# Three ones-matmul terms instead of four, with later reads and later row tails, in a masked-attention layer

## The chip, the cores and the metric

The kernel runs on one core of a Trainium2 chip. The metric is device time in microseconds (us) of one execution. The core has five engines that run their own instruction queues side by side: PE (TensorE, matrix products), DVE (VectorE), ACT (ScalarE), POOL (GpSimd) and SP (SyncE, which here only starts transfers). Transfers run on 16 DMA engines that all queues share. A transfer that adds into its destination is started by POOL.

## The reference

Eight graphs (F = 8) of 2048 nodes with 256 channels go through one layer of masked attention with 8 heads of 32 channels, then a feed-forward block, and a last residual norm. All is float32. Cut to what matters:

```python
qkv = einsum('fnc,ck->fnk', x, w_qkv)
scores = where(adj > 0, einsum('fnhd,fmhd->fhnm', q, k) / sqrt(D), -1e9)
attn = softmax(scores, axis=-1)
t = einsum('fhnm,fmhd->fnhd', attn, v).reshape(F, N, C)
y = layernorm(x + t, ln1_g, ln1_b)
f_out = relu(y @ w1 + b1) @ w2 + b2
out = layernorm(x + layernorm(y + f_out, ln2_g, ln2_b))
```

The softmax's denominator is the sum of exp(score) over all 2048 nodes m. How that sum is made is what the change is about.

## The kernel before

**Items and groups.** The work is cut into 1024 items `(f, qc, g, mb)`: graph, chunk of 512 query nodes, group of four heads, block of 128 key nodes. The 16 items of one `(f, qc, g)` are called a group here; there are 64. A group with g = 0 is called even, one with g = 1 odd. Item t is step t of the main loop (L552 to L578).

**One step.** PE makes the scores of item t + 2, four matmuls for four heads (L230), into PSUM. DVE adds the mask to them in two halves and writes a tile `p` of 128 x 2048 float32 in SBUF (L233). ACT takes the exponential of item t + 1 in place (L237). PE multiplies the exponentials of item t with the values V and adds the products up over the 16 blocks (L249). Tiles `p` come from a pool of 12.

**The denominator.** The 16 exponential tiles of a group must be summed over blocks and over the 128 nodes of each. PE does the second with a matrix of ones (L310), one "term" of four matmuls for each tile that it is given. To give it few tiles, the tiles are summed first, in `add_up` (L264): blocks 3, 6, 8, 11, 13 and 15 are added into block 0 by POOL (L271, constant `POOLED`); blocks 4, 7 and 10 into block 1, and 5, 9 and 12 into block 2, by accumulating transfers of 1 MB that POOL starts (L268, constant `MOVED`). Block 14 is left as it is (`ALONE`). The heads of these chains and block 14 are four terms. In the very last group, blocks 13 and 15 (`ENDED`) are terms of their own as well. Each addition into a head, by POOL or by a transfer, must wait for the addition before it into the same head.

**Side work.** All else on PE is "side work": generators that yield where they want a PSUM bank (`BANK`), more of the same bank (`MORE`), or a wait of some steps (a positive number). `advance(t)` (L457) runs once a step ahead of the scores. It resumes the generator that holds a bank first, then takes the others in the order of their due times. A credit of 2200 a step against 2048 for a unit of 512 columns in four matmuls means one unit a step, unless the step has reached the due time of something that waits: then it goes on. At most one bank is begun in a step. `start(t, gen, due)` enters a generator with its first step and its due time.

**What the change touches.** `denominator` (L295) reads the terms; it is started two steps after the group's last item and holds back its last term until the step `ready`, four after that item. `outcome` (L328) then divides (L345) and lets a transfer add the input rows to y (L334). `tail` (L349) is started with begin + 10 and due at begin + 26, where begin is six steps after the odd group's last item; it normalises y (`norm`, POOL's small instructions L282 to L286), goes through `feed_forward` (transposes, POOL's L412 and L414, the products with w1 and w2), normalises, multiplies and adds on POOL (L355, L357), adds the input rows by a transfer (L359), normalises and stores. `turn` (L169) loads rows of the next graph, transposes them and stores them as `xd`; `reload` (L191) loads those back. Both wait five steps between the load and its use. `pp` is the pool of `p`, `ld` that of the inputs, of three.

POOL and SP run their instructions in the order of the program: for each step, what `advance` emits comes ahead of what `add_up` emits.

Of the kernel before, what the change touches and what calls it, by code (L numbers as in the profile page):

```python
# [61 lines left out]
def fast_path(ctx, tc, cst, x, adj, out, RS):  # L62
# [106 lines left out]
    def turn(f, c):  # L169
        yield INPUTS - 2  # L170
        xc, xT = take([P, TPC, C], F32), take([P, 2, CH], F32)
        nc.sync.dma_start(xc, x[f, c * CH:(c + 1) * CH, :].rearrange("(j p) c -> p j c", p=P))
        yield 5
        yield from turn_rows(xc, xT)
        give(xc)
        yield 1
        nc.sync.dma_start(XD[f][c], xT)
        XT[f, c] = xT
        give(xT)
# [11 lines left out]
    def reload(f, c):  # L191
        while (f, c) not in XT:
            yield 1
        yield INPUTS - 1
        xT = take([P, 2, CH], F32)
        nc.sync.dma_start(xT, XD[f][c])
        yield 5
        return xT

    def project(f, c, g, xT=None):  # L200
# [19 lines left out]
    PT, O, OT, RC = {}, {}, {}, {}  # L220
# [33 lines left out]

    POOLED = (0, 3, 6, 8, 11, 13, 15)
    MOVED = ((1, 4, 7, 10), (2, 5, 9, 12))
    ALONE = 14

    ENDED = (13, 15)
    SUM = 4

    def add_up(item):  # L264
# [29 lines left out]

    def denominator(f, qc, g, ready):  # L295
        grp = (f, qc, g)
        terms = [PT.pop((f, qc, g, ALONE))] + [PT.pop((f, qc, g, chain[0])) for chain in MOVED + (POOLED,)]
        if (f, qc, g) == items[-1][:3]:
            terms[3:3] = [PT.pop((f, qc, g, b)) for b in ENDED]
        yield BANK  # L300
        ps = bank()
        for n, term in enumerate(terms):
            if n:
                yield MORE
            while n == len(terms) - 1 and state["now"] < ready:
                yield WAIT
            state["credit"] -= 4 * CH
            for h in range(4):
                r = D * h
                nc.tensor.matmul(ps[r:r + D, :], cst["ones"], term[:, h, :], start=(n == 0), stop=(n == len(terms) - 1))  # L310
        dT = op.tile([P, CH], F32, name="dT")
        nc.scalar.copy(dT, ps)
        yield 1
        yield BANK
        ps = bank()
        transposes(ps, [dT[:, j::TPC] for j in range(TPC)])
        if g == 0:
            RC[f, qc] = op.tile([P, TPC, H], F32, name="rc")
        rc = RC[f, qc]
        den = ps.rearrange("p (j c) -> p j c", c=P)[:, :, ::D]  # L320
        nc.vector.reciprocal(rc[:, :, 4 * g:4 * g + 4], den)
        nc.vector.tensor_tensor(RS[:, 0], RS[:, 0], den, ALU.add)
        nc.vector.tensor_tensor(RS[:, 1], RS[:, 1], den, ALU.min)
        if g == 1:
            begin = items.index((f, qc, g, LAST)) + SUM + 2
            start(begin, outcome(f, qc) if (f, qc) != (F - 1, NCK - 1) else finish(f, qc), begin)

    def outcome(f, qc):  # L328
        yield ROOM
        state["tails"] += 1  # L330
        xin = x[f, qc * CH:(qc + 1) * CH, :].rearrange("(p j) c -> p j c", p=P)
        y = yp.tile([P, TPC, C], F32, name="y")
        yield from divide(f, qc, y)
        nc.gpsimd.dma_start(y, xin, accum_op=ALU.add)  # L334
        begin = items.index((f, qc, 1, LAST)) + SUM + 2
        start(begin + 10, tail(f, qc, y, xin), begin + 26)

    def divide(f, qc, y):
        rc = RC.pop((f, qc))
# [62 lines left out]
    def feed_forward(y):  # L402
        yield TURNED
        state["turned"] = True
        yT = work.tile([P, 2, CH], F32, name="turned")
        for a in range(2):
            yield BANK
            ps = bank()
            transposes(ps, [y[:, j, a * P:(a + 1) * P] for j in range(TPC)])
            nc.scalar.activation(yT[:, a, :], ps, AF.Identity, bias=cst["be1c"][:, a:a + 1], scale=cst["g1c"][:, a:a + 1])  # L410
        yield 1
        nc.gpsimd.tensor_tensor(y, y, rows(cst["g1r"]), ALU.mult)  # L412
        yield 1
        nc.gpsimd.tensor_tensor(y, y, rows(cst["be1b2r"]), ALU.add)  # L414
        hT = work.tile([P, 2, CH], F32, name="hT")
        for d in range(2):
            yield BANK
            ps = bank()
            for a in range(2):
                if a:  # L420
                    yield MORE
                columns(ps, w1s[:, a, d * P:(d + 1) * P], yT[:, a, :], start=(a == 0), stop=(a == 1))
            nc.scalar.activation(hT[:, d, :], ps, AF.Relu, bias=cst["b1s"][:, d:d + 1], scale=1.0)
        state["turned"] = False
        yield 1
        z = y
        for jj in range(0, TPC, 2):
            yield BANK
            ps = bank()
            for j in range(jj, jj + 2):  # L430
                if j > jj:
                    yield MORE
                for d in range(2):
                    columns(ps[:, (j - jj) * C:(j - jj + 1) * C], hT[:, d, j * P:(j + 1) * P], w2s[:, d, :],
                            start=(d == 0), stop=(d == 1))
            nc.vector.tensor_tensor(z[:, jj:jj + 2, :], ps.rearrange("p (b c) -> p b c", c=C), z[:, jj:jj + 2, :], ALU.add)  # L436
# [4 lines left out]
    def start(t, gen, due):  # L441
        fill.append([t, gen, 1, due])
        fill.sort(key=lambda e: e[3])
# [108 lines left out]
    for t, (f, qc, g, mb) in enumerate(items):  # L552
        if g == 1 and mb % 2 and (f + 1 < F or qc + 1 < NCK):
            load_mask(f + (qc + 1) // NCK, (qc + 1) % NCK, mb // 2)
        for what, *which in NEXT.get(t % FRAME, []):
            to = f if what is ask and which[0] else f + 1
            if to < F:
                at = (0, 0, 0) if what is turn else (which[0], 0, 0) if what is ask else (0, which[1], which[0] * TPC)
                start(t, what(to, *which), t + 3 * MB if what is turn else items.index((to, *at)) - LEAD - 1)
        if t == len(items) - MB // 2:  # L560
            state["rows"] = take([P, TPC, C], F32)
            nc.sync.dma_start(state["rows"], x[f, qc * CH:(qc + 1) * CH, :].rearrange("(p j) c -> p j c", p=P))
        if t:
            advance(t)

        if t + 1 < len(items):
            exponentials(items[t + 1])
        if t + LEAD < len(items):
            nf, _, ng, nmb = items[t + LEAD]
            t0 = t  # L570
            while (nf, nmb // TPC, ng) not in V:
                advance(t0, finish=True)
                t0 += 1
            scores(items[t + LEAD])
        values(items[t])
        add_up(items[t])
        if mb == LAST:
            start(t + 2, denominator(f, qc, g, t + SUM), t + SUM + 4)  # L578
    t = len(items)
    state["side"] = None  # L580
    while fill:
# [238 lines left out]
```

## Time and profile before

| | us |
|---|---|
| median of 3 runs | 3245.18 (3244.88 to 3248.27) |
| profiled execution, its time | 3242.05 |
| profiled execution, its span | 3240.0 |
| ACT exponentials, busy | 1956.3 |
| DVE mask additions, busy | 2410.5 |
| POOL additions of `p` (382), busy | 1829.5 |
| POOL transfer issues of `p` (384), busy | 360.1 |

The main loop runs from 98 to 3176 us of the span; there PE is busy 3012.0 us of 3078, DVE 2672.4, ACT 2386.0, POOL 2565.7, and the DMA engines have a mean busy share of 0.82. The transfers of POOL's queue take 67.2% of 16 engines' span and move 435.85 MB; SP's take 13.1% and move 149.98 MB. The granted PE clock is 1.00 throughout the loop.

A group row of such a page gives the line, engine and operation, the tiles that are written and read, their shape, the number of instructions, then the busy time and the mean of one in ns, and after the bar the idle time of that engine just ahead of them with what ended it. Matmuls of float32 appear twice in the records, so a term of four matmuls is eight of them. A wait is listed as engine, line, what ended it, the total in us, how often, and the longest.

### The profile page before, as it was taken

What the parts mean: (1) busy time and instruction counts of PE and PEld (TensorE: products, weight loads), DVE (VectorE), ACT (ScalarE), POOL (GpSimd) and SP (SyncE); (2) the same over time, 40 slices, a digit from 0 to 9 for tenths busy, and PEclk for the clock granted to TensorE, in tenths of its full rate; (3) what the DMA queues carried; (4) which work ended last, traced back from release to release, by engine and by line L of the source; (5) the groups of instructions that cost most, each with busy time, mean ns of one, the idle gap of its engine ahead of it and who ended that gap; (6) DMA issues with size and microseconds to landing.
All of it is one profiled execution on the core that took longest, in us unless ns stands there. A gap on an engine that the chain in (4) does not pass through costs nothing.

```text
span 3240.0 us, 68306 instructions
## 1 busy us (share of the span) xinstructions
PE 3101.0 (96%) x28948; PEld 976.0 (30%) x28948; DVE 2739.5 (85%) x3203; ACT 2435.5 (75%) x1937; POOL 2593.3 (80%) x1357
## 2 busy tenths in 40 slices
PE   7899999999999999999999999999999999998994
PEld 4222333323332233322333323323233323332221
DVE  4888888888888888888988888888888888888994
ACT  3667778778778777778777778777778777777773
POOL 0568888788878888788887888888888788878894
PEclk8899999999999999999999999999999999999997
DMA  9688779778879788788788879878788878877773
GB/s 322 147 179 190 182 175 202 176 174 200 181 176 205 171 190 193 158 195 200 177 181 175 184 181 220 177 167 197 175 192 194 180 171 201 181 171 160 168 160 78
DMA packets 153384, 591.57 MB, mean 183 GB/s; under 512 B 15056, under 2 KB 67792, under 8 KB 103920
## 3 DMA queue, kind: packets, MB, share of 16 engines
q0 software_dynamic: 64560, 435.85, 67.2%
q1 hardware_dynamic: 87696, 149.98, 13.1%
q8 instruction: 229, 3.75, 0.4%
q10 hardware_dynamic: 816, 1.31, 0.1%
q14 instruction: 83, 0.68, 0.1%
HBM read 146.67 MB, written 37.75 MB: 57 GB/s over the span
## 4 chain that ended last, share of the span: by engine, by line
PE 75%; DVE 8%; POOL 5%; DMA 4%; issue 4%; ACT 2%; DVEq 0%; ACTq 0%; POOLq 0%
PE s L230 28%; PE x L249 24%; PE x L54 13%; DVE p L233 6%; PE x L310 6%; PE x L95 4%; DMA p<-p 3%; POOL p L271 2%; ACT p L237 2%; DMA mask<-md 1%; POOL y L357 1%; DVE st L278 1%; POOL y L355 0%; POOL y L414 0%; POOL y L412 0%
## 5 line engine op out<-in xcount | busy, mean ns | idle before, releaser
L233 DVE TENSOR_TENSOR p<-s,mask 128x1024 f32<-128x1024 f32 x2048 | 2410.5, 1219 | 360.3 <-PE s L230 202.9
L237 ACT ACTIVATE p<-p 128x2048 f32<-128x2048 f32 x1024 | 1956.3, 1910 | 510.2 <-DVE p L233 456.7
L271 POOL TENSOR_TENSOR p<-p 128x2048 f32<-128x2048 f32 x382 | 1829.5, 4791 | 216.0 <-ACT p L237 213.8
L230 PE MATMUL s<-qT,kT 32*128 32x512 f32 x8192 | 1171.2, 641 | 34.1 <-DVE p L233 29.1
L249 PE MATMUL x<-p,v 128*32 128x512 f32 x8192 | 1092.9, 606 | 16.7 <-ACT p L237 16.7
L268 POOL DMA_DIRECT2D p<-p x384 | 360.1, 957 | 305.5 <-ACT p L237 95.5
L230 PEld LDWEIGHTS s<-qT,kT 32*128 32x128 f32 x8192 | 320.5, 183 | 637.8 <-DVE p L233 580.1
L249 PEld LDWEIGHTS x<-p,v 128*32 128x32 f32 x8192 | 161.3, 108 | 796.4 <-issue 302.6
L310 PE MATMUL x<-p,ones 128*32 128x512 f32 x2016 | 261.1, 594 | 15.9 <-POOL p L271 9.7
L289 ACT ACTIVATE y<-y,nb,rs 128x256 f32<-128x256 f32 x372 | 219.2, 590 | 46.1 <-POOL nb L286 46.1
L54 PE MATMUL x<-in,wqkv 128*32 128x512 f32 x1888 | 243.5, 592 | 0.0
L278 DVE BATCH_NORM_STATS2 st<-y 128x6 f32<-128x256 f32 x372 | 155.2, 417 | 6.2 <-DMA y<-in_x_dram 6.2
L54 PE MATMUL x<-w2s,hT 128*32 128x256 f32 x2048 | 122.8, 381 | 3.3 <-DVE y L436 2.3
L54 PE MATMUL x<-turned,w1s 128*32 128x512 f32 x992 | 122.9, 592 | 0.4 <-ACT in L166 0.4
L54 PEld LDWEIGHTS x<-wqkv,in 128*32 128x32 f32 x3584 | 102.2, 110 | 63.5 <-issue 59.0
L54 PE MATMUL x<-wqkv,in 128*32 128x128 f32 x3584 | 117.2, 273 | 0.0
L310 PEld LDWEIGHTS x<-p,ones 128*32 128x32 f32 x2016 | 64.1, 110 | 171.4 <-issue 136.0
L54 PEld LDWEIGHTS x<-in,wqkv 128*32 128x32 f32 x1888 | 61.7, 110 | 140.9 <-issue 113.7
L283 POOL TENSOR_TENSOR rs<-rs,mhalf 128x4 f32<-128x4 f32 x93 | 97.1, 1044 | 7.7
L54 PEld LDWEIGHTS x<-w2s,hT 128*32 128x32 f32 x2048 | 66.1, 110 | 76.5 <-issue 30.3
L414 POOL TENSOR_TENSOR y<-y,be1b2r 128x1024 f32<-128x1024 f32 x32 | 85.4, 2667 | 0.6
L355 POOL TENSOR_TENSOR y<-y,g2r 128x1024 f32<-128x1024 f32 x31 | 82.7, 2668 | 1.2 <-ACT y L289 1.2
(117 smaller groups left out, 1333.1 us busy)
## 6 DMA issues: line engine op xcount, KB each, us to landing
p<-p POOLq DMA_DIRECT2D x384, 1024.0 KB, 10.5
in<-xd SPq DMA_DIRECT2D x87, 512.0 KB, 10.7
mask<-md SPq DMA_DIRECT2D x248, 128.0 KB, 8.0
y<-in_x_dram POOLq DMA_DIRECT2D x62, 512.0 KB, 8.0
p<-in_adj_dram SPq DMA_DIRECT2D x16, 1024.0 KB, 9.7
out_dram<-y SPq DMA_DIRECT2D x31, 512.0 KB, 6.4
in<-in_x_dram SPq DMA_DIRECT2D x29, 512.0 KB, 15.9
xd<-in SPq DMA_DIRECT2D x28, 512.0 KB, 10.9
```

The lines of the kernel that those rows point to most:

```text
L54: nc.tensor.matmul(out[r:r + D], lhsT[:, r:r + D], rhs, start=start, stop=stop)
L95: nc.tensor.transpose(ps[:, j * P:(j + 1) * P], s, ident)
L230: nc.tensor.matmul(ps2[half][:, j, :], KT[f, mb // TPC, g][r:r + D, (mb % TPC) * P:(mb % TPC + 1) * P], QT[f, qc, g][r:r + D, :], start=Tr ...
L233: nc.vector.tensor_tensor(pt[:, 2 * half:2 * half + 2, :], ps, MK[f, qc, mb // 2][:, mb % 2, None, :].to_broadcast([P, 2, CH]), ALU.add)
L237: nc.scalar.activation(PT[item], PT[item], AF.Exp, scale=1.0 / math.sqrt(D))
L249: nc.tensor.matmul(O[grp][r:r + D, :], V[f, mb // TPC, g][:, mb % TPC, r:r + D], PT[item][:, h, :], start=(mb == 0), stop=(mb == LAST))
L268: nc.gpsimd.dma_start(PT[f, qc, g, chain[0]], PT.pop(item), accum_op=ALU.add)
L271: nc.gpsimd.tensor_tensor(first, first, PT.pop(item), ALU.add)
L278: nc.vector.bn_stats(st, t[:, j, :])
L283: nc.gpsimd.tensor_tensor(rs, rs, cst["mhalf"], ALU.pow)
L289: nc.scalar.activation(t[:, j, :], t[:, j, :], AF.Identity, bias=nb[:, j:j + 1], scale=rs[:, j:j + 1])
L310: nc.tensor.matmul(ps[r:r + D, :], cst["ones"], term[:, h, :], start=(n == 0), stop=(n == len(terms) - 1))
```

## The change

Five things, all of them constants:

- `POOLED` takes block 14 in place of 13; block 13 goes to the end of the chain of block 1, as a fourth transfer of that chain; there is no block alone. The two chains change places in the tuple. `ENDED` is (14, 15).
- `denominator` has three terms, in the order block 2's chain, block 1's chain, block 0's; it starts four steps after the last item and holds its last term until six steps after it. Its due time stays.
- `tail` is due six steps later.
- In `feed_forward`, two steps instead of one between the products with w1 and those with w2.
- The wait between load and use is eight steps in `turn` and six in `reload`.

```diff
@@ turn @@
-        yield 5
+        yield 8
@@ reload @@
-        yield 5
+        yield 6
@@ add_up's constants @@
-    POOLED = (0, 3, 6, 8, 11, 13, 15)
-    MOVED = ((1, 4, 7, 10), (2, 5, 9, 12))
-    ALONE = 14
-
-    ENDED = (13, 15)
+    POOLED = (0, 3, 6, 8, 11, 14, 15)
+    MOVED = ((2, 5, 9, 12), (1, 4, 7, 10, 13))
+
+    ENDED = (14, 15)
@@ denominator @@
-        terms = [PT.pop((f, qc, g, ALONE))] + [PT.pop((f, qc, g, chain[0])) for chain in MOVED + (POOLED,)]
+        terms = [PT.pop((f, qc, g, chain[0])) for chain in MOVED + (POOLED,)]
         if (f, qc, g) == items[-1][:3]:
-            terms[3:3] = [PT.pop((f, qc, g, b)) for b in ENDED]
+            terms[2:2] = [PT.pop((f, qc, g, b)) for b in ENDED]
@@ outcome @@
-        start(begin + 10, tail(f, qc, y, xin), begin + 26)
+        start(begin + 10, tail(f, qc, y, xin), begin + 32)
@@ feed_forward @@
         state["turned"] = False
-        yield 1
+        yield 2
@@ main loop @@
-            start(t + 2, denominator(f, qc, g, t + SUM), t + SUM + 4)
+            start(t + SUM, denominator(f, qc, g, t + SUM + 2), t + SUM + 4)
```

## The prediction

> **What bounds the kernel now.** I read the page first, then the waits of POOL, then the order of time on PE and on POOL, and last the busy shares of short stretches. The page: its first part, the chain that ended last, one group and one DMA row.
>
> ```profile
> PE 3101.0 (96%) x28948; PEld 976.0 (30%) x28948; DVE 2739.5 (85%) x3203; ACT 2435.5 (75%) x1937; POOL 2593.3 (80%) x1357
> ...
> PE 75%; DVE 8%; POOL 5%; DMA 4%; issue 4%; ACT 2%; DVEq 0%; ACTq 0%; POOLq 0%
> ...
> L310 PE MATMUL x<-p,ones 128*32 128x512 f32 x2016 | 261.1, 594 | 15.9 <-POOL p L271 9.7 <-DMA p<-p 6.1
> ...
> p<-p POOLq DMA_DIRECT2D x384, 1024.0 KB, 10.5
> ```
>
> PE is busy 96% and carries 75% of the chain. That names the bound on average, and it is where the change removes work. PE's order of time shows what one removed term is worth:
>
> ```profile
> 1783.57 1.06 PE L249 MATMUL x<-p,v 128*32 128x512 f32 x8
> 1784.46 1.04 PE L310 MATMUL x<-p,ones 128*32 128x512 f32 x8
> 1785.43 1.14 PE L230 MATMUL s<-qT,kT 32*128 32x512 f32 x8
> 1786.50 1.06 PE L249 MATMUL x<-p,v 128*32 128x512 f32 x8
> ```
>
> A step is scores, values and one unit of side work: 2.93 us from score to score (1782.50 to 1785.43), of which scores and values take 2.07 in the merged chain (1.07 and 1.00) and the unit 0.86. But the second bound stands close behind it, and the averages hide it. POOL's waits:
>
> ```profile
> POOL p L271 <- ACT p L237: 213.8, 77, 85.5
> ...
> POOL p L268 <- DMA p<-p: 79.0, 33, 5.4
> ```
>
> The second row matters: a transfer L268 waits for the transfer three or four blocks earlier in its own chain, since both add into the same head, and POOL stands still meanwhile. One group of 16 blocks on POOL (columns: start, duration, what, idle before it):
>
> ```profile
> 1861.91 0.86 POOL L268 DMA_DIRECT2D p<-p  x1 [0.64 <-ACT y L289]
> 1862.47 4.91 POOL L271 TENSOR_TENSOR p<-p 128x2048 f32<-128x2048 f32 x1
> 1871.66 0.88 POOL L268 DMA_DIRECT2D p<-p  x1 [4.28 <-issue]
> 1872.25 2.69 POOL L355 TENSOR_TENSOR y<-y,g2r 128x1024 f32<-128x1024 f32 x1
> 1874.58 4.85 POOL L271 TENSOR_TENSOR p<-p 128x2048 f32<-128x2048 f32 x1
> 1879.11 2.67 POOL L357 TENSOR_TENSOR y<-y,be2r 128x1024 f32<-128x1024 f32 x1
> 1882.08 0.88 POOL L359 DMA_DIRECT2D y<-in_x_dram  x1 [0.30 <-POOL y L357]
> 1882.70 4.86 POOL L271 TENSOR_TENSOR p<-p 128x2048 f32<-128x2048 f32 x1
> 1887.64 0.19 POOL L282 TENSOR_SCALAR rs<-mv 128x4 f32<-128x4 f32 x1
> ...
> 1889.47 4.57 POOL L271 TENSOR_TENSOR p<-p 128x2048 f32<-128x2048 f32 x1
> 1893.97 1.85 POOL L268 DMA_DIRECT2D p<-p  x2
> ```
>
> In order: transfer of block 10, addition of 11, 4.28 us idle, transfer of 12 (block 9 landed at 1871.1), additions of 13 and 15, the next group's addition of 3, its transfers of 4 and 5. The DMA side of the end of it:
>
> ```profile
> core 0: us, PE busy (x) PEld busy (x) DVE busy (x) ACT busy (x) POOL busy (x), PEclk, DMA share, GB/s
> ...
> 1884.00:1887.00 3.00, 2.49 (x20) 0.47 (x16) 2.17 (x3) 1.91 (x1) 3.00 (x1) 1.00 1.01 201
> 1887.00:1890.00 3.00, 2.39 (x20) 0.63 (x24) 1.09 (x2) 1.26 (x2) 2.66 (x6) 1.00 0.20 55
> 1890.00:1893.00 3.00, 3.00 (x28) 1.15 (x24) 2.88 (x6) 2.29 (x3) 3.00 (x1) 1.00 0.00 0
> ```
>
> The DMA engines are full while a group's transfers run, then empty (0.00) until POOL reaches the next transfer of 4. So there is a loop that takes turns between two resources: transfers 4 to 9 on full DMA engines, a wait of POOL for a landing, three additions, transfer of 4 again.
>
> **What the Trainium skill says.** "DMA: Bandwidth & Descriptors", Rules for kernel authors: an accumulating DMA reads its destination and writes it later with nothing held in between, so the earlier DMA's semaphore must be waited for. The 79.0 us row is that wait. The same page, Issuing engines are not separate DMA queues: all run on the same 16 engines; the share of 1.01 above agrees. "TensorE: Matmul & The Clock Gate", Part 1, Architectural detail: GpSimd's queue is strictly first in, first out, so what follows a waiting transfer waits too; the additions behind the 4.28 us agree. "GPSIMD Engine Reference", 3.1: 4497 ns for such an addition; the trace has 4791 (4.5 apart when back to back), and I use the trace's.
>
> **The change part by part.**
>
> Term 14 alone goes: 64 groups lose one unit, 64 x 0.86 = 55 us of PE. Where a step then holds no unit, the two DVE additions of 1219 ns bound it at 2.44, and 0.49 is saved instead. So PE's own floor falls by 31 to 55 us, to about 3190.
>
> Block 13 becomes a transfer: 64 more of 1 MB. The transfers of POOL's queue take 67.2% of 3240 us for 435.85 MB, so 5.2 us for 1.05 MB. DMA share in the loop rises from 0.82 by 64 x 5.2 / 3078 = 0.11 to 0.93. The issue costs POOL 0.6 to 0.96 each (957 mean, 0.6 to the next instruction): 38 to 61 us. POOL's additions stay at six, now with 14 in place of 13.
>
> The new wait is the main point. Transfer 13 adds into head 1 and waits for transfer 10; behind it on POOL stand the additions of 14, 15 and the next 3, then the transfer of 4, which starts the next group's DMA work. Until now the last wait was 12 for 9. In the trace block 10 lands one transfer after 9: 1876.8 against 1871.1. From that landing I count to the next transfer of 4: 0.5 to notice, 0.6 issue, three additions 14.3, plus the tail's work in between.
>
> The tail's place: its due time moves from step 15 of the odd group (LAST + 32) to step 5 of the next even one. Until now w1 and w2 were forced two units a step and w2 ended near step 1; now they go singly, with one step more between them, and w2 ends near step 5. Eleven steps of norm and yields later come L355, L357 and L359: from steps 12 to 15 to steps 16 to 18. In program order that is behind addition 15, out of the wait's cover: 2.3 + 2.7 more. y's transfer (0.6) and the four small ones of a norm (1.9) are between as before. Even group: 0.5 + 0.6 + 14.3 + 5.0 + 0.6 + 1.9 = 22.9. Odd group: L412 and L414 fall before transfer 13, in the wait; 14.9 (additions joined without a DMA: 13.7).
>
> From transfer 4 to block 10's landing the trace has a mean of 34.8 us in even groups (31.1 to 37.8; y's 512 KB is among them) and 32.3 in odd ones (29.6 to 34.6). New loop: 57.7 + 47.2 = 104.9 for two groups. Now it is 49.5 + 47.3 = 96.8. So +8.0 with transfers as traced and the tail where I count it. Two things the trace can't say. SP's loads may move into the gap and shorten the stretch: with the shortest seen, 31.1 and 29.6, two groups take 6.4 less. And I count the tail's steps from the code; if its two multiplications still find cover, 5.0 less. So +8.0 at one end and -3.4 at the other, where PE's own gain of 1.7 for two groups would take over; I take the middle, +2.3. Times 31.5 pairs: +72. Once, about 9 us of lag is taken up before PE waits: the POOLED term is now read 19.0 us after block 15's exponential and its addition ends 10.7 to 12.4 after it, and it moves two steps later. Sum: +63.
>
> The terms start at t + 4 and the last at t + 6. The chain heads are read two steps later (5.9 us), which covers 13's later landing (about 5.7 behind 12's) at today's pace, not an added lag per group. Their buffers come free later; twelve are there, and I count 9 to 11 in use. The longer waits in `turn` (8) and `reload` (6) cost nothing while side work fills every step and inputs are due a dozen steps later. SP's store of xd moves three steps later, and SP's reloads queue behind it; without that cover a block's units are forced, say one 0.86 for each of 28 turned pieces and 87 reloads, 99 us; I take 0. Swapping the chains in MOVED only orders the reads: the chain that ends with 12 first.
>
> Sum against the profiled execution's 3242.05: 3305. The median shown is 3 us higher: 3308.
>
> **The rivals.** (1) The same loop at its worst end: +8.0 x 31.5 - 9 = +243, 3488. For it: the stretch repeats with the position in the frame within 1 us, so its loads are the program's own, and the order on POOL is the program's. Against it: SP's loads have 13.1% of the engines' time and the gap is new room for them. (2) A buffer: block 13's landing, some 6 us later than 12's, gates DVE's write of block 6 of the next group if buffers are handed out in order of release. Priced at 1.5 us a group less PE's gain: 96 - 55, 3286. For it: exponentials end only 1.0 to 1.3 us before values read them. Against it: DVE waits for POOL's transfers 4.3 us in all today. (3) The other side, faster: the wait of 13 is filled by work that POOL must do anyway, so the loop stays under PE's: 3245 - 55 = 3190. It decides from the point where the loop of two groups falls below PE's 96.8 - 1.7 = 95.1; with stretches as traced it is 104.9, so 9.8 us of them, or of the tail's work behind transfer 13, must move. PE's 75% of the chain speaks for it, and the 5 to 7 us for which POOL stands idle between its transfers of 4 and 12, which the tail could use; against it, the shortest stretches seen still give 98.5 with the tail where I count it. (4) The two cancel within 0.2%, which is about 6 us and what a measurement can tell from no change.
>
> **How the numbers follow.** Forecast 0.52 (its own range 3255 to 3400); rival 1 0.16; rival 2 0.10; rival 3 0.16; cancelling 0.06. Slower 0.78, same 0.06, faster 0.16. The range is 3230 to 3445: it leaves out most of rival 3 and the upper part of rival 1.
>
> **What would show it.** POOL's waits for DMA p<-p at L268 grow from 79.0 to 200 us or more, and the idle stands ahead of transfer 13. L310 or DVE begin to wait for POOL and DMA; PE's share falls below 95%; L355 and L357 come after the addition of 15. DMA share near 0.90. It is wrong if L268's waits stay near 79, or if PE stays at 96% with a shorter span: then the gap was covered.

## The result and the profile after

The changed kernel takes 3528.1 us (median of four runs, 3522.6 to 3531.7) against 3246.7 us before on the same chip: a ratio of 1.0865, with a 95% interval of 1.0846 to 1.0884. That is 281 us slower, well above the forecast of 3308 us and above its range, which ended at 3445. The profiled execution's span is 3523.7 us. In the code of the changed kernel the lines from 260 on stand one lower: the transfers are L267, POOL's additions L270, the norm's POOL instructions L281 to L285, ACT's part of the norm L288, the terms L309, the division L344, the tail's multiplication and addition L354 and L356, those of `feed_forward` L411 and L413.

The page of the changed kernel, busy shares, the chain that ended last, the group of the terms and the transfers:

```profile
PE 3134.8 (89%) x28436; PEld 976.2 (28%) x28436; DVE 2732.9 (78%) x3203; ACT 2431.2 (69%) x1937; POOL 2648.1 (75%) x1421
...
DMA 3%; POOL 3%; PE 3%; issue 1%; DVE 1%; ACT 1%; POOLq 0%; ACTq 0%; DVEq 0%
...
L309 PE MATMUL x<-p,ones 128*32 128x512 f32 x1512 | 193.2, 596 | 18.2 <-DMA p<-p 18.1
...
p<-p POOLq DMA_DIRECT2D x448, 1024.0 KB, 10.8
```

PE fell from 96% to 89%, and no other engine rose: ACT and DVE have the same work spread over more time, and POOL, which got 64 issues more, has a smaller share as well. The engines' work has hardly grown; they wait for each other more. The chain that ended last was followed back through some 12% of the span only, so this time it names no bound. The term did go (1512 matmul records for 2016, 193.2 us for 261.1), and a transfer still takes about as long from issue to landing (10.8 us, 10.5 before). The waits of the changed kernel, all engines, say where the time is (engine, line, what ended it, total us, times, longest):

```profile
ACT y L288 <- POOL nb L285: 245.2, 46, 14.4
POOL p L267 <- DMA p<-p: 211.3, 83, 6.7
...
POOL p L267 <- issue: 123.8, 52, 7.4
...
PE x L249 <- ACT p L237: 108.0, 30, 9.5
...
PE s L230 <- DVE p L233: 100.8, 151, 3.3
```

The same waits of ACT and PE before:

```profile
ACT y L289 <- POOL nb L286: 46.1, 16, 9.3
...
PE s L230 <- DVE p L233: 29.1, 65, 1.4
...
PE x L249 <- ACT p L237: 16.7, 11, 5.1
```

Two rows stand out, not one. POOL's wait for landings is the row that the forecast announced (79.0 before). It is not where it was announced: split by block, 4.3 of its 211.3 us stand ahead of transfer 13, the rest ahead of earlier transfers. The wait ahead of 13 is there all the same, listed under other names. Counted from the landings (POOL idle for more than 0.3 us ahead of a transfer that starts within 1 us of the landing before it in its chain), it comes to 194.5 us in 45 of the 64 groups; the wait ahead of 12, the last one before, went from 57.6 to 10.7 us, the one ahead of 10 from 151.5 to 182.3.

The largest row was small before: ACT stands at its part of the norm for POOL's `nb`, 245.2 us against 46.1. ACT takes its instructions in order, so the exponentials stand behind it; PE's wait for them went from 16.7 to 108.0.

**The even groups.** POOL in one even group, in order of time (start, duration, what, idle before it):

```profile
2015.91 1.58 POOL L267 DMA_DIRECT2D p<-p  x1
2024.88 0.85 POOL L267 DMA_DIRECT2D p<-p  x1 [7.39 <-issue]
2025.45 9.52 POOL L270 TENSOR_TENSOR p<-p 128x2048 f32<-128x2048 f32 x2
2034.95 2.35 POOL L354 TENSOR_TENSOR y<-y,g2r 128x1024 f32<-128x1024 f32 x1
2037.37 2.36 POOL L356 TENSOR_TENSOR y<-y,be2r 128x1024 f32<-128x1024 f32 x1
2040.03 0.89 POOL L358 DMA_DIRECT2D y<-in_x_dram  x1 [0.30 <-POOL y L356]
...
2042.81 4.57 POOL L270 TENSOR_TENSOR p<-p 128x2048 f32<-128x2048 f32 x1
2047.33 1.83 POOL L267 DMA_DIRECT2D p<-p  x2
```

The transfer of 12 is issued at 2015.91, and POOL then stands for 7.39 us until block 10 has landed (2024.4 in the records of the transfers; the row puts the wait down to "issue", the same wait under another name). Behind the transfer of 13 come the additions of 14 and 15, both tail instructions, the row transfer, the norm's four small ones, the next group's addition of 3, and only then its transfer of 4. The DMA engines meanwhile, in four stretches of the same time:

```profile
core 0: us, PE busy (x) PEld busy (x) DVE busy (x) ACT busy (x) POOL busy (x), PEclk, DMA share, GB/s
...
2032.00:2036.00 4.00, 3.52 (x32) 0.71 (x24) 3.69 (x5) 3.10 (x2) 4.00 (x2) 1.00 0.99 218
2036.00:2040.00 4.00, 2.18 (x12) 0.52 (x16) 1.00 (x1) 2.25 (x2) 3.65 (x2) 0.70 0.21 67
...
2044.00:2048.00 4.00, 4.00 (x36) 1.36 (x36) 3.34 (x6) 3.78 (x4) 4.00 (x3) 1.00 0.21 41
2048.00:2052.00 4.00, 4.00 (x40) 0.96 (x36) 3.50 (x4) 3.31 (x4) 4.00 (x3) 1.00 1.03 251
```

They are full until 13 has nearly landed (2037.8), almost empty (0.21) while POOL works, but for the 512 KB of the tail's rows in the stretch left out (2040 to 2044), and full again from the transfer of 4. That is the forecast's loop.

**The odd groups.** POOL at the end of an odd group, and ACT at the same time:

```profile
1971.26 0.87 POOL L267 DMA_DIRECT2D p<-p  x1 [0.95 <-ACT p L237]
1971.84 9.43 POOL L270 TENSOR_TENSOR p<-p 128x2048 f32<-128x2048 f32 x2
1981.36 0.19 POOL L281 TENSOR_SCALAR rs<-mv 128x4 f32<-128x4 f32 x1
...
1983.03 0.19 POOL L285 TENSOR_SCALAR nb<-nb 128x4 f32<-128x4 f32 x1
1985.73 4.54 POOL L270 TENSOR_TENSOR p<-p 128x2048 f32<-128x2048 f32 x1 [2.52 <-ACT p L237]
1990.21 1.83 POOL L267 DMA_DIRECT2D p<-p  x2
```

```profile
1968.38 1.91 ACT L237 ACTIVATE p<-p 128x2048 f32<-128x2048 f32 x1 [1.30 <-DVE p L233]
1983.26 0.60 ACT L288 ACTIVATE y<-y,nb,rs 128x256 f32<-128x256 f32 x1 [12.97 <-POOL nb L285]
1983.76 1.89 ACT L237 ACTIVATE p<-p 128x2048 f32<-128x2048 f32 x1
```

Here the last norm of the tail has its POOL part behind the transfer of 13 and both additions. ACT stands 12.97 us for it. After it the roles turn round: POOL stands 2.52 us for the exponential of block 3, which ACT could not make earlier. For a part of this stretch PE does nothing at all:

```profile
1976.00:1980.00 4.00, 1.84 (x20) 0.47 (x12) 2.83 (x4) 0.00 (x0) 3.92 (x2) 0.98 0.94 197
1980.00:1984.00 4.00, 0.00 (x0) 0.00 (x0) 0.33 (x1) 0.74 (x2) 2.88 (x5) 0.88 0.16 33
1984.00:1988.00 4.00, 2.29 (x16) 0.76 (x20) 0.00 (x0) 4.00 (x4) 2.27 (x1) 0.50 0.01 4
```

(The columns are those of the windows above.) From 1980 to 1984 PE is idle and nearly all else too; POOL is busy for 2.88 of the 4.00 us. In the whole trace ACT has 17 such waits of over 5 us, all in odd groups. POOL's wait behind them, for the exponential of block 3, is much rarer: 20.5 us in all over the groups 4 to 59.

### The profile page after: what moved, and what is told of

It is laid out like the page before. It is cut to its first block, busy times and chain, and to the rows that moved or that the text cites. A ratio compares the mean times of both kernels' runs of the same rounds, so it can differ in the third digit from the quotient of the medians.

```text
span 3523.7 us, 67543 instructions
## 1 busy us (share of the span) xinstructions
PE 3134.8 (89%) x28436; PEld 976.2 (28%) x28436; DVE 2732.9 (78%) x3203; ACT 2431.2 (69%) x1937; POOL 2648.1 (75%) x1421
## 5 line engine op out<-in xcount | busy, mean ns | idle before, releaser
L270 POOL TENSOR_TENSOR p<-p 128x2048 f32<-128x2048 f32 x382 | 1831.7, 4797 | 174.0 <-ACT p L237 169.5
L230 PE MATMUL s<-qT,kT 32*128 32x512 f32 x8192 | 1188.2, 650 | 107.2 <-DVE p L233 100.8
L249 PE MATMUL x<-p,v 128*32 128x512 f32 x8192 | 1121.2, 620 | 177.0 <-ACT p L237 108.0
L267 POOL DMA_DIRECT2D p<-p x448 | 426.4, 994 | 548.3 <-DMA p<-p 211.3
L288 ACT ACTIVATE y<-y,nb,rs 128x256 f32<-128x256 f32 x372 | 220.4, 594 | 245.2 <-POOL nb L285 245.2
L54 PE MATMUL x<-in,wqkv 128*32 128x512 f32 x1888 | 244.4, 594 | 0.1
L309 PE MATMUL x<-p,ones 128*32 128x512 f32 x1512 | 193.2, 596 | 18.2 <-DMA p<-p 18.1
L54 PE MATMUL x<-turned,w1s 128*32 128x512 f32 x992 | 142.2, 648 | 0.0
L54 PE MATMUL x<-w2s,hT 128*32 128x256 f32 x2048 | 137.3, 403 | 1.1 <-ACT oT L253 0.7
L54 PE MATMUL x<-wqkv,in 128*32 128x128 f32 x3584 | 121.2, 282 | 15.8 <-DVE y L344 15.8
L54 PEld LDWEIGHTS x<-wqkv,in 128*32 128x32 f32 x3584 | 106.1, 114 | 69.9 <-issue 47.4
L282 POOL TENSOR_TENSOR rs<-rs,mhalf 128x4 f32<-128x4 f32 x93 | 96.1, 1033 | 7.7
L54 PEld LDWEIGHTS x<-in,wqkv 128*32 128x32 f32 x1888 | 61.3, 110 | 142.0 <-issue 121.3
L54 PEld LDWEIGHTS x<-w2s,hT 128*32 128x32 f32 x2048 | 69.8, 117 | 96.3 <-issue 61.6
L309 PEld LDWEIGHTS x<-p,ones 128*32 128x32 f32 x1512 | 48.0, 110 | 136.9 <-issue 94.2
L311 ACT COPY dT<-x 128x512 f32<-128x512 f32 x63 | 36.9, 586 | 68.2 <-PE x L309 68.1
L413 POOL TENSOR_TENSOR y<-y,be1b2r 128x1024 f32<-128x1024 f32 x32 | 82.3, 2573 | 0.6
## 6 DMA issues: line engine op xcount, KB each, us to landing
p<-p POOLq DMA_DIRECT2D x448, 1024.0 KB, 10.8
```

Of the source, the lines that this page charges most:

```text
L54: nc.tensor.matmul(out[r:r + D], lhsT[:, r:r + D], rhs, start=start, stop=stop)
L230: nc.tensor.matmul(ps2[half][:, j, :], KT[f, mb // TPC, g][r:r + D, (mb % TPC) * P:(mb % TPC + 1) * P], QT[f, qc, g][r:r + D, :], start=Tr ...
L249: nc.tensor.matmul(O[grp][r:r + D, :], V[f, mb // TPC, g][:, mb % TPC, r:r + D], PT[item][:, h, :], start=(mb == 0), stop=(mb == LAST))
L267: nc.gpsimd.dma_start(PT[f, qc, g, chain[0]], PT.pop(item), accum_op=ALU.add)
L270: nc.gpsimd.tensor_tensor(first, first, PT.pop(item), ALU.add)
L282: nc.gpsimd.tensor_tensor(rs, rs, cst["mhalf"], ALU.pow)
```

## The experiments

All kernels were timed over four runs (`y_turn_only` over twelve) beside the kernel before; ratios are given with their 95% intervals. In the expectations, "loop theory" is the forecast's mechanism; "ACT theory" and, in later ones, "norm theory" mean that ACT's wait for the norm is the cost; "DMA theory" means the fuller DMA engines, and "buffer theory" that tiles are held longer and their next writer waits.

I read every trace in the same way: from the issue of the transfer of 4 to the landing on which the group's last waiting transfer depends, and from that landing to the next group's transfer of 4, as means over the groups 4 to 59. The four legs of a pair add up to its period, so the sum only restates the time (both ends of the run are left out; 31.5 times the difference to the pair before gives the difference of the medians within 26 us); how it is split is the finding.

| kernel | landing of block | even: to landing, to next 4 | odd: to landing, to next 4 | pair | median us |
|---|---|---|---|---|---|
| before | 9 | 28.0, 21.6 | 26.0, 21.4 | 97.0 | 3247 |
| changed | 10 | 31.5, 23.1 | 32.2, 19.2 | 106.0 | 3528 |
| a_tail_back | 10 | 33.6, 19.2 | 31.4, 17.6 | 101.8 | 3390 |
| b_tail_only | 9 | 26.4, 27.6 | 28.1, 23.6 | 105.7 | 3495 |
| n_tail_norm_early | 9 | 25.2, 26.6 | 27.9, 21.6 | 101.3 | 3367 |
| q_changed_norm_early | 10 | 31.4, 22.9 | 32.7, 17.6 | 104.6 | 3481 |
| x_tail_loads_back | 10 | 33.0, 18.9 | 31.2, 15.7 | 98.8 | 3303 |
| w_late13_loads_back | 10 | 33.4, 17.1 | 31.4, 16.0 | 97.9 | 3275 |
| f_behind12 | 12 | 40.1, 19.1 | 38.1, 16.3 | 113.6 | 3754 |

**The tail put back.** The changed kernel with the tail's two times as before:

```diff
-        start(begin + 10, tail(f, qc, y, xin), begin + 32)
+        start(begin + 10, tail(f, qc, y, xin), begin + 26)
...
-        yield 2
+        yield 1
```

> The changed kernel with the tail's due time (begin + 26) and the step between the feed-forward products (1) of before; the three terms and the transfer of block 13 stay. Loop theory (transfer 13 waits for block 10's landing, and all that stands behind it on POOL sets the group's length): the two multiplications go back into the wait's cover, 5.0 us for two groups, 3528 - 157 = about 3370. ACT theory (POOL is late, and the last norm's ACT instructions wait for POOL's nb and hold the exponentials up): the last norm's POOL work falls ahead of transfer 12 again, ACT's wait for nb goes from 245 back to some 50 us, about 3330. DMA theory (the added 1 MB a group fills the DMA engines, and that alone is the price): about 3500 or more.

3390.4 us, ratio 1.0445 (1.0423 to 1.0466). The tail's times are worth 138 us of the 281 here, 4.2 us a pair by the legs; the loop theory had 157 us. ACT's wait for `nb` fell from 245.2 to 84.8 us, POOL's for landings from 211.3 to 117.4. What is left, 145 us, belongs to chains, terms and loads.

**The tail alone.** The kernel before with only these two times changed.

> The kernel before with only the tail's due time (begin + 32) and the two steps between the feed-forward products of the change. Loop theory: the last wait is still 12 for 9, and the multiplications come behind it, 27.5 + 22.9 = 50.4 us against 49.5 in even groups and little in odd ones: 3275 to 3310. ACT theory: the last norm comes behind transfer 12 and its additions, ACT's wait for nb rises by 100 us or more: 3350 to 3450. DMA theory: no transfer is added, 3247.

3495.3 us, ratio 1.0771 (1.0753 to 1.0789). It lies above every range that was named: no transfer of 13, no term less, and still 250 us. So the two halves do not add (145 and 250 against 281 for both). The waits and POOL's order of time of this kernel:

```profile
ACT y L289 <- POOL nb L286: 217.9, 26, 11.8
...
POOL p L268 <- DMA p<-p: 176.6, 51, 6.0
PE x L249 <- ACT p L237: 148.1, 23, 10.4
```

```profile
1955.97 1.01 POOL L268 DMA_DIRECT2D p<-p  x1
1956.56 2.82 POOL L414 TENSOR_TENSOR y<-y,be1b2r 128x1024 f32<-128x1024 f32 x1
1958.88 9.58 POOL L271 TENSOR_TENSOR p<-p 128x2048 f32<-128x2048 f32 x2
1968.55 0.19 POOL L282 TENSOR_SCALAR rs<-mv 128x4 f32<-128x4 f32 x1
```

The norm's first instruction L282 stands behind the transfer of 12 and the additions of 13 and 15, as it does in the changed kernel behind 13, 14 and 15. The later tail brings the same order about without the new chain. In the even groups L355 and L357 stand behind the addition of 15 as well: the stretch from the landing to the next transfer of 4 grew from 21.6 to 27.6 us, in the odd ones from 21.4 to 23.6. DVE writes a tile `p` anew only when the transfer that read it has landed; its wait for that grew as well, from 4.3 to 100.6 us. Whether the pool of 12 tiles is a bound of its own here was not tried.

**The norm's second half later.** The changed kernel with seven steps in place of two between POOL's and ACT's part of the last norm, so that ACT would reach it after `nb` is there:

```diff
-        yield from norm(z)
+        yield from norm(z, 7)
```

> The changed kernel with seven steps instead of two between POOL's nb and ACT's use of it in the last norm of a tail alone; nothing depends on that norm but the store. Loop theory: POOL's order and its waits stay, no gain, 3500 to 3530. ACT theory: of the 245 us that ACT waits for nb, the some 215 that are the last norm's go: about 3310. DMA theory: no gain.

3562.9 us, ratio 1.0976 (1.0956 to 1.0996), slower than the changed kernel. ACT's wait is gone (20.4 us), but the result rows are stored five steps later, and `y` has two buffers:

```profile
DVE y L344 <- DMA out_dram<-y: 95.4, 23, 8.9
```

The next division waits for the store, 95.4 us of it, and DVE's wait for the landings of `p` grew from 51.2 to 141.4 us. One wait was swapped for another, so this run says nothing on what ACT's wait costs.

**The norm's first half earlier.** The other way to part them: the wait ahead of the last norm cut, once on the tail alone and once on the changed kernel.

```diff
         nc.gpsimd.dma_start(z, xin, accum_op=ALU.add)
-        yield 7
+        yield 3
         yield from norm(z)
```

> The kernel before with the tail's two new times (due at begin + 32, two steps between the feed-forward products) and the wait ahead of the tail's last norm cut from 7 steps to 3, so that its four small POOL instructions stand some four steps earlier, ahead of the transfer of block 12 and of the additions of 13 and 15. Norm theory (what the later tail costs is ACT standing at the last norm for POOL's rs and nb, with the exponentials behind it): ACT's wait at L289 for POOL's nb falls from 217.9 us to under 90, and the time from 3495 to 3250 to 3340. Loop theory (the cost is POOL's L355 and L357 behind addition 15): these stay where they are, so the time stays at 3430 to 3500. Buffer theory (y or the exponentials' buffers are held longer whatever the norm does): 3400 to 3500 with ACT's wait gone.

> The changed kernel with the wait ahead of the tail's last norm cut from 7 steps to 3. Loop theory (transfer 13's wait and the tail's multiplications behind addition 15 set 57 us for each even group): the even groups keep their 57 us, and only the odd ones can gain; 3440 to 3520. Norm theory alone: ACT's wait at L288 falls from 245 us to under 110 and the time by about as much, to 3370 to 3430. Both bind together, each in its own group of the pair: ACT's wait falls but the time lands at 3430 to 3480. Buffer theory: no gain, 3500 to 3560.

With the tail alone: 3367.0 us, ratio 1.0370 (1.0348 to 1.0392), 128 us less than 3495.3. The whole last norm stands four steps earlier, with POOL's four instructions of 0.2 to 1.0 us, ACT's part and the store, and half of the tail's cost went. The store is not the reason: nothing waits for it in either kernel with the tail alone. With the whole change: 3481.1, ratio 1.0722 (1.0700 to 1.0744), 47 us less. ACT's waits fell to 61.1 and 50.9 us. The lines of the first, where the tail's cost was larger:

```profile
POOL p L268 <- DMA p<-p: 178.9, 57, 6.5
...
PE s L230 <- DVE p L233: 111.1, 112, 6.6
...
ACT y L289 <- POOL nb L286: 61.1, 22, 8.6
```

POOL's wait for landings is the same as in the tail alone (178.9 and 176.6), and the stretch behind it in the even groups keeps 26.6 of 27.6 us: that half of the cost is not the norm. In the changed kernel the even groups keep 22.9 of 23.1 us, while the odd ones fall from 19.2 to 17.6. So the place of the norm is a cost of its own, in the odd groups, beside the loop in the even ones. Not all of it is ACT's stall: of the 1.6 us, 0.75 are the norm's own time on POOL, which no longer stands behind the landing, and 0.85 are POOL's idle time, nearly all of it the wait for an exponential. Neither theory alone gave both times: the loop theory's 3440 to 3520 holds for the second run but its 3430 to 3500 not for the first, the norm theory missed both. The outcome in which both bind, each in its own group, had 3430 to 3480 for the second, and 3481 is at its upper edge.

**Each half of the tail's delay.** The kernel before with the due time alone, and with the extra step alone.

> The kernel before with the tail due at begin + 32 and nothing else. Norm theory: the due time is what moves the last norm past the transfer of 12 and the additions, so nearly all of the tail's cost is here: 3400 to 3500, ACT's wait for nb 150 us or more. Loop theory: 3275 to 3310. If the extra step between the products is the cost: 3247 to 3270.

> The kernel before with two steps in place of one between the feed-forward products and nothing else. Norm theory: one step moves the last norm only from about steps 11 and 12 to 12 and 13 of the odd group, still ahead of the transfer of 12: 3247 to 3290, ACT's wait for nb under 80 us. If the two parts of the tail's delay simply add (3495 less 3355 from the run with the due time alone): 3380 to 3400.

3355.0 (ratio 1.0329, 1.0311 to 1.0348) and 3336.8 us (1.0279, 1.0254 to 1.0304). Both missed: the due time cost less than the norm theory said, and one single step cost 90 us where next to nothing was expected. ACT's wait is 114.4 us in the first and 93.5 in the second, from 46.1. In the second PE also waits 51.9 us for rows of the next graph that ACT has still to copy (L54 for L166), a sign that the side work changes its order as a whole when one of its generators is shifted. 108 and 90 add to 198 of the 250 us for both.

**Block 13 as a term of its own.** The changed kernel without the seventh transfer; block 13 is read as a fourth term.

```diff
-    MOVED = ((2, 5, 9, 12), (1, 4, 7, 10, 13))
+    MOVED = ((2, 5, 9, 12), (1, 4, 7, 10))
+    ALONE = 13
```

> The changed kernel with block 13 left alone as a fourth term, so with no transfer of 13; POOLED, the later terms and the later tail stay. Loop theory: the last wait is 12 for 9 again: 3275 to 3310. ACT theory: POOL is late by one transfer less, but the last norm still stands behind 12: 3300 to 3400. DMA theory: all of the loss goes, about 3250.

3473.5 us, ratio 1.0705 (1.0687 to 1.0723), above all three ranges. Only 55 us come back, with one term more for PE, and DVE's wait for landings goes from 51.2 to 122.5 us. The time is close to that of the tail alone (3495), which has the same wait of 12 for 9 and the same late tail. So 64 transfers of 1 MB are not the main part of the price, and as long as the tail is late, taking the wait of 13 away leaves most of the loss; the loop theory as I had put it (3275 to 3310) missed here.

**The chains and later terms alone,** with tail and load waits as before, and the same with the transfer of 13 issued behind the addition of 15, its chain read last and one step later:

> The kernel before with the change's chains and later terms alone: tail and both load waits as before. Loop theory with the forecast's own numbers, without the tail's two multiplications: 52.7 + 47.2 = 99.9 us for a pair of groups against 96.8, times 31.5 less 9 = +89, so 3320 to 3350, and POOL's wait for landings at 100 us or more. If transfer 13 is covered: 3190 to 3240. If the chains are the whole cost of the run with the tail put back, and the longer loads cost nothing there: 3380 to 3400.

> The same with the transfer of block 13 issued behind the addition of 15 and its chain read last, one step later. Loop theory: 10 us of additions leave the stretch between block 10's landing and the next transfer of 4, so it falls under PE's pace, and one term per group is saved: 3190 to 3250. If the 64 more transfers cost by themselves, through fuller DMA engines or held buffers: 3260 to 3320, with DVE's wait for landings at L233 at 40 us or more.

```diff
             if mb in chain[1:]:
-                nc.gpsimd.dma_start(PT[f, qc, g, chain[0]], PT.pop(item), accum_op=ALU.add)
+                if mb != 13:
+                    nc.gpsimd.dma_start(PT[f, qc, g, chain[0]], PT.pop(item), accum_op=ALU.add)
...
+        if mb == LAST:
+            nc.gpsimd.dma_start(PT[f, qc, g, 1], PT.pop((f, qc, g, 13)), accum_op=ALU.add)
```

3302.9 us (1.0180, 1.0163 to 1.0197) and 3274.6 (1.0096, 1.0079 to 1.0113). The first is what the forecast was really about: its legs of 18.9 and 15.7 us to the next transfer of 4 were forecast at 17.9 (22.9 less the tail's 5.0) and 14.9, the other two, 33.0 and 31.2, at 34.8 and 32.3, and the period of 98.8 at 99.9. That is a rise of 1.8 us a pair where 3.1 were forecast, and 57 us in all where 3320 to 3350 meant 74 or more. Moving one issue behind two additions, with its chain read last and a step later, took 28 us off, where the loop theory had 3190 to 3250. The time lies in the range for fuller DMA engines or held buffers (3260 to 3320), with DVE's wait below the 40 us that was named for it; neither was tried by itself. The floor of 3190 is not reached by either. In the second DVE waits 33.6 us for landings, PE 66.1 us for DVE and 36.2 us for input rows:

```profile
PE s L230 <- DVE p L233: 66.1, 118, 4.0
...
PE x L95 <- DMA in<-in_x_dram: 36.2, 6, 6.6
...
DVE p L233 <- DMA p<-p: 33.6, 15, 5.0
```

**The same issue moved with the longer loads, and with the whole change.**

> The changed kernel with the tail's two times put back (due begin + 26, one step) and the transfer of block 13 issued after the addition of block 15 rather than ahead of addition 14, its chain read last by the terms and one step later. All bytes and terms of the change stay; only POOL's wait for block 10's landing now has the additions of 14 and 15 ahead of it. Loop theory: 10 us of additions leave the loop, which falls under PE's: 3190 to 3270, POOL's wait for landings under 60 us. If the fuller DMA engines are the price: 3370 to 3400 as with transfer 13 in its place. If held buffers are: 3300 to 3400 with DVE's wait for POOL and DMA at 100 us or more.

> The changed kernel, tail as changed, with the transfer of block 13 issued behind the addition of 15, its chain read last and one step later. Loop theory alone (even groups bound by the wait of 13 with additions and the tail's two multiplications behind it): 10 us leave every group's loop, 3528 less 250 or more, 3230 to 3290. Norm theory alone: nothing changes in the last norm's place, so ACT's wait for nb stays at 200 us or more and the time at 3440 to 3500. Both, each in its own group of a pair: the even groups gain, the odd ones keep ACT's stall; 3420 to 3480. Which of the two comes out is read from the step times of even and odd groups.

3324.4 (1.0231, 1.0210 to 1.0252), 66 us under the run with the tail put back, and 3494.9 us (1.0759, 1.0738 to 1.0779), only 33 us under the changed kernel. The first is above the loop theory's 3190 to 3270. It lies in the range for held buffers, 3300 to 3400, but with 70.4 us of DVE's wait for landings where 100 were named; that rival stays open. In the second ACT's wait for `nb` stayed at 169.7 us. The better place of 13 is worth half as much when the late tail stands behind the wait anyway; the time lies above the 3420 to 3480 that "both" gave and at the upper end of the norm theory's 3440 to 3500.

**A dose of the loop.** The tail put back, and block 13 added to the other chain, where it must wait for the transfer of 12:

```diff
-    MOVED = ((2, 5, 9, 12), (1, 4, 7, 10, 13))
+    MOVED = ((2, 5, 9, 12, 13), (1, 4, 7, 10))
```

> The changed kernel with its tail put back, and block 13 appended to the other chain: it adds into head 2 and waits for the transfer of 12, which itself starts only after 9 has landed. A dose: block 12 lands some 6 us after 10, and the additions of 14 and 15 still stand behind the wait. Loop theory: +5 to +6 us in each of 63 groups over the run with the tail put back (3390), some 3640 to 3760, and POOL's wait for landings at L267 at 350 us or more. If the transfer's wait is not in the loop: 3370 to 3420.

3753.7 us, ratio 1.1566 (1.1547 to 1.1585): 363 us more than with the tail put back, 5.8 us for each of 63 groups, where 5 to 6 were expected. Same instructions, same bytes, one landing later. The first leg, now to the landing of 12, grew (33.6 to 40.1, 31.4 to 38.1); the second did not (19.1, 16.3). The loop sets the pace: 13.2 us more of landing in a pair made it 11.8 us longer. The waits of this kernel are also a lesson in reading:

```profile
POOL p L267 <- issue: 430.3, 88, 14.4
...
PE x L309 <- DMA p<-p: 296.6, 49, 11.6
...
POOL p L267 <- DMA p<-p: 93.2, 44, 11.4
```

The expected 350 us at L267 stand there, but under "issue"; the row of the landing alone has 93.2. What a transfer waits for is better read from the landings. PE's 296.6 us for the chain head, which lands later and is read first, might be a rival cause of the added time. The second leg speaks against it: POOL has 0.5 us idle there in even groups and 0.2 in odd ones, and next to none of that for an exponential, so its work from the landing to the next transfer of 4 was not held up by PE.

**Later terms, longer loads, and each load wait.**

> The kernel before with the terms of the denominator started four steps after a group's last block rather than two, and the last one read no sooner than six steps after rather than four; chains, loads and tail as before. The forecast's step (covered, cost nothing): 3240 to 3260. Buffer theory (three chain heads and block 14 are held two steps longer, so DVE waits for a buffer): 3270 to 3330, with DVE's wait at L233 for POOL and DMA at 30 us or more. If only 12 us of lag in each group went: faster, 3200 to 3235.

> The kernel before with the two longer waits for loads (8 in turn, 6 in reload) and nothing else. The forecast's step: nothing, 3240 to 3255. If the forced units are the price that the forecast named and left out: 3280 to 3350. If inputs held longer help the loads' order: under 3235.

> The kernel before with the wait in turn at 8 steps and that in reload at 5 as before. If the store of xd, three steps later, and the loads queued behind it on SP are what the run with both longer waits showed (3306): 3290 to 3320. If the 87 reloads are: 3240 to 3260. The forecast gave both nothing.

> The chains and later terms with transfer 13 behind addition 15, the tail and the wait in reload as before, but the wait in turn at 8 steps. With it at 5 (3275), PE waits 36 us at L95 for the rows that turn loads. If the longer wait is there for just that, and the reload's wait was the harm: 3235 to 3260. If the turn's wait is itself the harm: 3290 to 3330, as in the run with both (3324).

The kernel before with later terms alone: 3285.7 us (1.0119, 1.0100 to 1.0138). With both longer load waits: 3306.0 (1.0171, 1.0149 to 1.0193). With the wait in `turn` alone: 3247.9 (1.0001, 0.9992 to 1.0010), no change. So the one step more in `reload` carries the 59 us, by difference; it was not run alone. In the run with both DVE began to wait for landings:

```profile
POOL p L268 <- DMA p<-p: 103.9, 43, 4.7
...
DVE p L233 <- DMA p<-p: 52.2, 14, 7.4
```

(79.0 and 4.3 before), all of it at the same two blocks, 9 and 10 of odd groups, seven times each. That the loads' transfers, shifted by a step, meet POOL's there fits this but was not tried by itself. For the later terms DVE's wait for landings is 7.7 us, so the 30 us that were named as the sign of held buffers did not come. The last run puts the wait in `turn` at 8 on the best arrangement of chains: 3290.9 us (1.0134, 1.0114 to 1.0153) instead of 3274.6, so there that wait is not free. No version beat the kernel before.

## Why the forecast was wrong

**Right: the direction and the place of the wait.** POOL waits ahead of transfer 13 for 194.5 us by the landings, L354 and L356 stand behind the addition of 15, PE's share fell below 95%, and the dose run shows that the loop binds. The row that was named, 200 us or more, came to 211.3 by luck, since the wait ahead of 13 is hardly in it; and the DMA engines' share in the loop is 0.85, not near 0.90. From 10's landing to the next transfer of 4 in even groups the forecast had 22.9 us, item by item; it is 23.1: 0.6 to the issue, additions 13.7, the tail's two 4.7, the norm 1.6, issues 1.5, idle 1.1. Part of this agreement is luck as well: additions, tail and norm came out 1.2 us below the forecast's items, and it had nothing for idle time. One landing was misread: 10 landed at 1878.2, not at 1876.8, but no term of the sum rests on it.

**Wrong: "I take the middle, +2.3".** The forecast had an end at which the stretches stay as traced (+8.0 for two groups) and an end with the shortest stretches and the tail under cover (-3.4), and went to the middle of them. Measured: 106.0 - 97.0 = +9.0. Term by term from the end of 104.9:

| term | forecast, as traced | changed kernel |
|---|---|---|
| even: transfer 4 to landing of 10 | 34.8 (shortest 31.1) | 31.5 |
| even: landing to next 4 | 22.9 | 23.1 |
| odd: transfer 4 to landing of 10 | 32.3 (shortest 29.6) | 32.2 |
| odd: landing to next 4 | 14.9 | 19.2 |

Of the three reliefs that the low end counted, one came, the even stretch (-3.3). The odd stretch did not shorten, and the tail's two multiplications found no cover. Against that stands a term of which the forecast had nothing: +4.3 us in the odd groups. There it said "L412 and L414 fall before transfer 13, in the wait"; in the changed kernel 2.2 us of them come behind it on average. The last norm's small instructions add 0.75, idle time 0.97, of which the wait for the exponential of block 3 is a part, and a slower start of 13 some 0.3. The middle between two ends would have needed a reason for meeting halfway; the trace offered none. The forecast's own argument for the traced end, that the stretch repeats by position, held for the odd groups and not for the even ones. The first rival, 3488 us, came within 40 us; it was given a chance of 0.16. Its +8.0 is near the +9.0 in part by luck: it had neither the -3.3 of the even stretch nor the +4.3 of the odd groups, and the two nearly cancel.

**Wrong in part: what moves with the tail.** The forecast had the tail at 5.0 us a pair without cover and at nothing with it. Within the whole change 5.0 was near (4.2 us, 138 in all); the middle gave half of it away. The place was off, though: of what went with the tail put back, 1.6 us a pair are in the odd stretch, for which the forecast had nothing. And alone the same two times cost 8.7 us a pair, which no end of the forecast gives.

Of the moved steps the forecast followed POOL's long instructions to their new place. It counted the norm's four short ones as 1.9 us of POOL, in even groups only, and did not ask who waits for them. ACT does, in order, with the exponentials behind it: 217.9 us in the run of the tail alone. Moving that norm four steps earlier took 157 us of ACT's wait away and gave 128 us back there; in the changed kernel it took 194 us away and gave 47, about half of it POOL's idle time. So ACT's wait of 245.2 us is not 245 us of the kernel's time. The section that the forecast cited from the Trainium skill for GpSimd ("TensorE: Matmul & The Clock Gate", Part 1, Architectural detail) names the scalar engine's queue in the same place as strictly first in, first out; the 12.97 us stall with an exponential right behind it agrees.

**Wrong: "cost nothing".** For the longer waits in `turn` and `reload` the forecast named a price without cover, 99 us, and took 0; for `turn` alone that was right; `reload` cost 59 by difference. The later terms were "not an added lag per group"; alone they cost 39 us.

**How the 281 us come together.** In one order of adding: chains and later terms +57, longer loads +87, the later tail +138. Alone the loads cost 59 and the tail 250; the sum of 57, 59 and 250, 366 us, is more than the whole, and that the late tail and the loop of 13 lengthen the same stretch fits this. What stays open is why one step of `reload` or one step in the tail costs as much as it does. The traces show where the waits appear, but not a single cause for each.

## What to carry to other kernels

When a step is moved in a schedule of in-order queues, follow its short instructions too: ask for each who waits for it and what is queued behind that waiter, because 1.6 us of small operations behind two additions stopped the exponentials for 13 us. Then ask how much of that wait the bound sees: of 157 us less of it 128 reached the time in one kernel, of 194 only 47 in the other. Where two resources take turns, write down the loop leg by leg for each kind of group, and give each leg a value with a reason of its own, not the middle between two ends. In a kernel whose first engine is at 96%, no shift of a step is free until the trace names what hides it: here four of five shifts by one to six steps cost 39 to 108 us each, alone (the one in `reload` by difference).

## What the hardware showed that was not expected

PE's busy time rose although it had less to do: 3134.8 us for 28436 matmul records against 3101.0 for 28948, where the removed terms are worth 55 us by the forecast's sum. The granted clock, the share of its full rate that PE was given, fits this: it is 0.957 on average (0.987 before), and in the windows above it falls to 0.50 just after the stretch in which PE was idle. The Trainium skill ("TensorE: Matmul & The Clock Gate", Part 1, What's actually happening) says that the gate goes to half rate after an idle window; the 0.50 agrees. In the dose run with the longest stalls PE was busy for 3192.9 us at 0.925. So a stall of PE also makes matmuls after it slower (the means of scores and values are 650 and 620 ns, 641 and 606 before). Whether that lengthened the kernel, in which PE had time to spare, no run shows.
